# Dense passes in fp32 instead of two fp32r halves, and layer 2's counted nodes from 2304 to 2560

## The chip, the core and the metric

The kernel runs on one core of a Trainium2 chip. TensorE (PE in the profile, its weight loads PEld) multiplies, VectorE (DVE) and ScalarE (ACT) work element by element, GpSimd (POOL) issues the gathers of rows by index, and SyncE (SP) issues the plain transfers. The time is device microseconds of one execution, and a comparison is made on medians of several runs.

## The reference

A two-layer GraphSAGE network with a residual layer norm, on 12500 nodes of 256 features and 200000 edges that are sorted by destination:

```python
def _sage_conv(x, src, dst, W_l, b_l, W_r):
    msgs = x[src]
    agg = jax.ops.segment_sum(msgs, dst, num_segments=N_NODES)
    deg = jax.ops.segment_sum(jnp.ones((src.shape[0],), x.dtype), dst, num_segments=N_NODES)
    mean = agg / jnp.maximum(deg, 1.0)[:, None]
    return mean @ W_l + b_l + x @ W_r

h = jax.nn.relu(_sage_conv(x, src, dst, W1_l, b1, W1_r))
h = jax.nn.relu(_sage_conv(h, src, dst, W2_l, b2, W2_r))
return _layernorm(x + (h @ W3 + b3))
```

Destinations are drawn as `12500 * u**2`, so low-numbered nodes have many more edges than high-numbered ones.

## The kernel before, in words

All 12500 nodes stand in 98 blocks (NB) of 128. The edges stand in 1563 tiles of 128. Sums over edges are made in two ways.

**Gathered nodes.** For nodes from HOT1 = 1792 on (layer 1) or HOT2 = 2304 on (layer 2), a round of `Gathers` (line 258) issues four indirect DMAs on POOL (line 286), one tile of edges each; four products with 0/1 matrices (line 298, 32 output rows each) sum the rows, and for each group of one or two rounds two further products (line 314) put the sums at their nodes, and VectorE adds them to a ring of sums (line 328).

**Counted, or hot, nodes.** For the nodes below that, the kernel counts how often each of the 12500 source nodes occurs for each of 512 or 256 hot nodes: `count` (line 881) makes 0/1 matrices on VectorE (lines 898, 908), multiplies them on TensorE in bf16 (lines 930, 934) and copies the result as bytes (line 944 on ScalarE, line 948 on VectorE). COUNTED (line 109) lists the six groups of nodes. A dense pass, `products` (line 841), then multiplies all rows of x (or h) by such a table: for each of 98 blocks, ScalarE widens the counts from bytes (`widened`, line 833), SP loads the block's rows (`loaded`, line 775), and TensorE accumulates over all blocks in PSUM. A full pass is 512 columns wide, with one PSUM bank for each half of the features (dense_ps and beside_ps, line 868); a half pass is 256 wide (line 864).

**Exactness.** Before, the dense passes multiply in the fp32r form, and each row of x and h is split in two parts for it: the upper 20 bits of each word, by an integer mask of -4096, and the rest, by a subtraction. The products of both parts are added in PSUM, which is 2 parts x 2 halves of the features, four matmuls a block. x is split by `splitting` (line 784) in layer 1's first stage: SP loads two blocks, VectorE masks and subtracts (lines 812 and 813), SP stores them to x2_d. h is split in each `first_block` by `exact` (line 758, called at 1184) and stored to h2_d, beside h itself in h_d. Dense passes read x2_d and h2_d, 256 KB a block.

**Order.** PE and POOL run in an order written out by hand in `layer` (line 645). It loops over the gather rounds; after each round's gathers it lets pieces of finished blocks pass (`pieces`: transposes, line 1094; the two weight products, lines 1123 and 1125; in layer 2 also line 1207) and fills with dense work (`fill`) until the planned cost of the round reaches `room_for`. The planned cost of one block of a dense pass is `product_cost` (line 993); counts, gathers and blocks have planned costs as well. `stages_1` and `stages_2` (lines 1055 and 1067) say which passes, counts and moves are mixed in which stage: layer 1 has one half pass (nodes 1536 to 1791) and three full ones, layer 2 four full ones and one half (2048 to 2303). When the fill is used up, the last rounds run without it, `left` of them, and the last blocks are drained.

The split stage of layer 1 mixes three things: the counts of group 3, `degrees`, and `splitting`.

Of the kernel before, what the change touches and what calls it, by code (L numbers as in the profile page):

```python
# [8 lines left out]
F32 = mybir.dt.float32  # L9
F32R = mybir.dt.float32r  # L10
# [17 lines left out]
P = 128  # L28
# [23 lines left out]
def by_runs(  # L52
# [56 lines left out]
    COUNTED = [(0, 512), (512, 1024), (1024, 1536), (1536, 1792), (1792, 2048), (2048, 2304)]  # L109
    HOT1, HOT2, N1 = 1792, 2304, 4  # L110
# [32 lines left out]
    x2_d = dram.tile([P, NB, 2, D], F32, name="x2_d")  # L143
    h2_d = dram.tile([P, NB, 2, D], F32, name="h2_d")
# [473 lines left out]
    split = keep.tile([P, 2, 2, D], F32, name="split")  # L618
    assert NB * CW % 4 == 0
    counts_flat = [keep.tile([P, NB * CW], U8, name=f"counts{i}") for i in range(2)]  # L620
    counts = [t.rearrange("p (b d) -> p b d", b=NB) for t in counts_flat]
# [151 lines left out]
    N2, WIDE = 5, 4  # L773

    def loaded(b, back, table):

        rows = rows_pool.tile([P, 2, D], F32, name="rows", bufs=N2)
        load = nc.sync.dma_start(rows, table[:, b])
        freed(load, back)
        if table is h2_d:  # L780
            tc.add_manual_dep(load.ins, rows_after, LANDED, reason="the first layer's last gathers")
        return rows

    def splitting():

        size = 2 * 2 * D
        bufs = NB * CW // 4 // size
        flat = counts_flat[1].bitcast(F32)
        raw = {}

        def fetched(u):
            t = flat[:, u // 2 % bufs * size:(u // 2 % bufs + 1) * size].rearrange("p (b k d) -> p b k d", b=2, k=2)
            whole = min(2, (N - u * P) // P)
            loads = []
            if whole < 2:
                left = N - (u + whole) * P
                nc.vector.memset(t[:, whole, 1], 0.0)
                loads.append(nc.sync.dma_start(t[:left, whole, 1], x[(u + whole) * P:N]))
            if whole:
                loads.append(nc.sync.dma_start(t[:, :whole, 1], x[u * P:(u + whole) * P].rearrange(  # L800
                    "(b p) d -> p b d", p=P)))
            if u < 2 * bufs:
                for load in loads:
                    tc.add_manual_dep(load.ins, strips[-1], LANDED, reason="the gathers' tables first")
            return t

        for b in range(0, NB, 2):
            for u in range(b, min(b + 2 * (bufs - 3), NB), 2):
                if u not in raw:
                    raw[u] = fetched(u)  # L810
            s = raw.pop(b)
            nc.vector.tensor_scalar(s[:, :, 0].bitcast(I32), s[:, :, 1].bitcast(I32), -4096, None, op0=OP.bitwise_and)
            nc.vector.tensor_tensor(s[:, :, 1], s[:, :, 1], s[:, :, 0], op=OP.subtract)
            nc.sync.dma_start(x2_d[:, b:b + 2], s)
            yield COST_SPLIT
# [17 lines left out]
    def widened(counted):  # L833
        wide = rows_pool.tile([P, DN], F32, name="wide", bufs=WIDE)
        if len(counted.shape) > 2:
            nc.scalar.copy(wide.rearrange("p (b d) -> p b d", b=2).bitcast(F32R), counted)
        else:
            nc.scalar.copy(wide.bitcast(F32R), counted)  # L838
        return wide
# [777 lines left out]
```

## Time and profile before

| what | value |
|---|---|
| median of 3 runs | 3097.36 us (3088.63 to 3106.94) |
| the profiled execution's own time | 3104.8 us |
| its span | 3103.0 us |
| mean granted TensorE clock | 0.897 |
| gathers issued on POOL | 988 in layer 1, 908 in layer 2 |
| moved by DMA | 634.88 MB, 205 GB/s on the mean |

The page gives the busy time of each engine, then slices of the span with a digit for the busy share in tenths, then the chain of waits followed back from the last instruction. In a row of a group, the count (x) is of records in the trace, then busy time and the mean length of one, then the engine's idle time before them and what ended it. A matmul's length holds the run through the array as well, so matmuls that follow one another overlap, and the price of one in a stream is the distance between two starts. A row of windows gives, for each stretch, its length, each engine's busy time with the count of instructions, the granted clock as a share of the full one, and the share of DMA time.

### The profile page before, as it was taken

The page shows a single profiled execution, that of the slowest core. Times are in us where ns is not written, and L with a number is a line of the kernel's source. Part 1 is how long each engine was busy: PE and PEld are TensorE (multiplying, and loading weights), DVE is VectorE, ACT ScalarE, POOL GpSimd, SP SyncE. Part 2 cuts the span into 40 slices and gives each one's busy share as a digit, 9 for nine tenths or more (in the row PEclk, how much of TensorE's full clock was granted, in tenths as well). Part 3 has the DMA queues.
Part 4 walks back from the last instruction along what each step waited for, and adds up shares of the span by engine and source line. Part 5 has one row for each costly group of instructions (what it writes and reads, how often), then busy time and mean ns, then how long its engine had stood idle before and what let it go on. Part 6 is the DMA issues. An engine that isn't in the chain of part 4 may idle for free.

```text
span 3103.0 us, 45692 instructions
## 1 busy us (share of the span) xinstructions
PE 2412.6 (78%) x13753; PEld 1604.2 (52%) x13753; DVE 1525.2 (49%) x4554; ACT 1384.4 (45%) x2794; POOL 1851.4 (60%) x1906
## 2 busy tenths in 40 slices
PE   3356888888878788888876888887888888887776
PEld 1123555555544555556554555554555566566644
DVE  6764766656666666643232124444444343344344
ACT  0236666666622666644332443554444423333321
POOL 6546666556655666656654665665666556666653
PEclk7567999999999999989988998998998899989988
DMA  4893877756655555567756875766677657677843
GB/s 116 301 348 109 260 228 232 252 183 200 188 183 164 174 165 177 170 187 245 241 178 198 258 229 177 219 215 184 209 226 230 192 173 219 212 222 236 263 130 90
DMA packets 366615, 634.88 MB, mean 205 GB/s; under 512 B 85371, under 2 KB 173081, under 8 KB 366361
## 3 DMA queue, kind: packets, MB, share of 16 engines
q1 hardware_dynamic: 271011, 382.42, 38.3%
q0 software_dynamic: 91008, 248.63, 26.7%
q8 instruction: 115, 1.88, 0.2%
q10 hardware_dynamic: 4342, 0.80, 0.2%
q14 instruction: 139, 1.14, 0.1%
HBM read 544.85 MB, written 86.78 MB: 204 GB/s over the span
## 4 chain that ended last, share of the span: by engine, by line
PE 63%; issue 9%; DVE 8%; another core or an unknown queue 7%; DMA 6%; ACT 5%; DVEq 1%; POOL 0%; ACTq 0%; SPq 0%; POOLq 0%
PE dense_ps L868 10%; PE beside_ps L868 10%; PE count_ps L930 9%; PE part_ps L298 8%; PE block_ps L1123 5%; PE block_ps L1125 5%; PE sum_ps L314 5%; PE block_ps L1207 3%; PE block_ps L1094 3%; ACT counts L944 3%; PE dense_ps L864 3%; PE count_ps L934 2%; DMA rows<-h_d 2%; DMA x_d<-counts 1%
## 5 line engine op out<-in xcount | busy, mean ns | idle before, releaser
L286 POOL DMA_INDIRECT got<-in_x_dram,src_t x988 | 983.6, 996 | 646.1 <-issue 241.3
L286 POOL DMA_INDIRECT got<-h_d,src_t x908 | 865.6, 953 | 573.9 <-issue 226.4
L930 PE MATMUL count_ps<-pick,low 128*128 128x490 bf16 x1360 | 453.8, 376 | 333.8 <-ACT counts L944 139.1
L944 ACT CAST counts<-count_ps 128x490 f32 (+2 forms) x852 | 581.2, 682 | 232.3 <-PE count_ps L934 52.4
L868 PE MATMUL dense_ps<-wide,rows 128*128 128x512 f32 x1372 | 637.7, 465 | 46.5 <-ACT wide L838 16.3
L868 PE MATMUL beside_ps<-wide,rows 128*128 128x512 f32 x1372 | 565.7, 412 | 0.0
L838 ACT CAST wide<-counts 128x512 fp32r<-128x512 uint8 x588 | 359.6, 621 | 455.8 <-PE beside_ps L868 188.9
L868 PEld LDWEIGHTS dense_ps<-wide,rows 128*128 128x128 f32 x1372 | 276.6, 202 | 187.3 <-issue 99.5
L908 DVE TENSOR_SCALAR pick<-steps,tables 128x686 bf16<-128x686 f16 (+3 forms) x792 | 319.0, 416 | 105.2 <-PE count_ps L930 38.6
L298 PE MATMUL part_ps<-got,one 128*32 128x257 f32 (+1 forms) x3792 | 331.7, 424 | 22.8 <-DMA got<-h_d,src_t 12.4
L930 PEld LDWEIGHTS <-low 128*128 128x128 bf16 x1360 | 152.0, 117 | 318.2 <-issue 161.6
L948 DVE CAST counts<-count_ps 128x196 f32 (+2 forms) x316 | 208.5, 660 | 179.8 <-PE count_ps L930 46.9
L868 PEld LDWEIGHTS beside_ps<-wide,rows 128*128 128x128 f32 x1372 | 275.8, 201 | 40.1 <-ACT split L876 0.3
L308 ACT COPY some<-part_ps 128x257 f32<-128x257 f32 (+1 forms) x340 | 127.0, 374 | 351.1 <-PE part_ps L298 102.9
L314 PEld LDWEIGHTS sum_ps<-two,some 128*128 128x128 f32 x1360 | 223.7, 215 | 89.4 <-issue 39.4
L242 DVE TENSOR_TENSOR one<-lo_t,lane_b 128x128 f32<-128x128 bf16 x474 | 134.8, 286 | 267.1 <-PE part_ps L298 81.6
L314 PE MATMUL sum_ps<-two,some 128*128 128x128 f32 x1360 | 238.7, 303 | 32.2 <-ACT some L308 12.8
L328 DVE TENSOR_TENSOR sums<-sums,sum_ps 128x256 f32 x340 | 139.7, 411 | 250.0 <-PE beside_ps L868 88.7
L1133 DVE TENSOR_TENSOR own<-block_ps,biases 128x256 f32<-128x256 f32 x196 | 82.9, 423 | 312.3 <-remote 101.8
L298 PEld LDWEIGHTS part_ps<-got,one 128*32 128x32 f32 x3792 | 78.5, 112 | 191.1 <-issue 167.9
L934 PE MATMUL count_ps<-aft,low 128*128 128x98 bf16 x659 | 169.0, 256 | 0.0
L1130 ACT COPY sums<-zero 128x256 f32<-128x256 f32 x164 | 66.4, 405 | 224.6 <-PE block_ps L1125 74.3
(199 smaller groups left out, 2904.8 us busy)
## 6 DMA issues: line engine op xcount, KB each, us to landing
rows<-h_d SPq DMA_DIRECT2D x490, 256.0 KB
rows<-x_d SPq DMA_DIRECT2D x392, 256.0 KB
x_d<-counts SPq DMA_DIRECT2D x49, 512.0 KB
h_d<-split SPq DMA_DIRECT2D x98, 256.0 KB
got<-in_x_dram,src_t POOLq DMA_INDIRECT x988
got<-h_d,src_t POOLq DMA_INDIRECT x908
h_d<-own SPq DMA_DIRECT2D x98, 128.0 KB
h_sb<-h_d SPq DMA_DIRECT2D x98, 128.0 KB
```

The source lines that it names most:

```text
L286: rows = nc.gpsimd.indirect_dma_start(out=g[:, j, :D], out_offset=None, in_=self.table, in_offset=bass.IndirectOffsetOnAxis(ap=src_t[:, e: ...
L298: strip = nc.tensor.matmul(part_ps[j * W:(j + 1) * W, :width], lhsT=one[:, j], rhs=g[:, j, :width], start=r == 0, stop=r == n - 1)
L314: nc.tensor.matmul(sum_ps[:, c], lhsT=some[:, c * P:(c + 1) * P], rhs=two, start=True, stop=True)
L838: nc.scalar.copy(wide.bitcast(F32R), counted)
L868: nc.tensor.matmul(ps[c], lhsT=own, rhs=wide[u].bitcast(F32R), start=u + k == 0, stop=u == NB - 1 and k == 1)
L908: nc.vector.tensor_scalar(r[:, :w * NB], steps[:, :w * NB], key_t[g][:, t - lo_g:t - lo_g + 1], None, op0=OP.is_equal)
L930: nc.tensor.matmul(ps[:, :(b - a) * NB], lhsT=s, rhs=r[:, a * NB:b * NB], start=j == 0, stop=j == n_in - 1 and alone)
L934: nc.tensor.matmul(ps[:, :NB], lhsT=before[0], rhs=before[1], start=False, stop=True)
L944: copies.append(nc.scalar.copy(to[:, :, a:][:, :, bass.ds(off_act.at(t), b - a)], of).ins)
L948: beside.append(nc.vector.tensor_copy(to[:, :, a:][:, :, bass.ds(off_dve.at(t), b - a)], of).ins)
L1123: nc.tensor.matmul(ps[:, 1], lhsT=own_t[:, c], rhs=wr[:, c], start=c == 0, stop=c == NC - 1)
L1125: product = nc.tensor.matmul(ps[:, 0], lhsT=agg[:, c], rhs=wl[:, c], start=c == 0, stop=c == NC - 1)
```

## The change

- The dense passes read x and h_d themselves and multiply in fp32: two matmuls a block in place of four, with no cast to fp32r on either operand. The rows come two blocks to one transfer of 256 KB (five such pairs ahead).
- `splitting`, `exact` and both tables x2_d and h2_d go, with their VectorE operations, loads and stores. The count tables need no flat form any more, and `sums_b` and `w3_sb` get tiles of their own.
- The last group of counted nodes is 2048 to 2559, and HOT2 is 2560: layer 2's last pass is a full one of 512 columns, and layer 2 has fewer gather rounds.
- The planner's costs change: a product block 1.0 to 0.87 (half pass 0.6 to 0.45), the last piece of `first_block` 1.65 to 0.9 on VectorE, and `room_for` 5.05 to 4.65 in layer 1 and 5.0 to 5.05 in layer 2.

```diff
-    COUNTED = [(0, 512), (512, 1024), (1024, 1536), (1536, 1792), (1792, 2048), (2048, 2304)]
-    HOT1, HOT2, N1 = 1792, 2304, 4
+    COUNTED = [(0, 512), (512, 1024), (1024, 1536), (1536, 1792), (1792, 2048), (2048, 2560)]
+    HOT1, HOT2, N1 = 1792, 2560, 4
...
-    def exact(t, s):
-
-        nc.vector.tensor_scalar(s[:, 0].bitcast(I32), t.bitcast(I32), -4096, None, op0=OP.bitwise_and)
-        nc.vector.tensor_tensor(s[:, 1], t, s[:, 0], op=OP.subtract)
...
-    N2, WIDE = 5, 4
+    PAIRS_IN, WIDE = 5, 4
-    def loaded(b, back, table):
-
-        rows = rows_pool.tile([P, 2, D], F32, name="rows", bufs=N2)
-        load = nc.sync.dma_start(rows, table[:, b])
-        freed(load, back)
+    def loaded(u, since, table):
+
+        rows = rows_pool.tile([P, 2, D], F32, name="rows", bufs=PAIRS_IN)
...
+            loads.append(nc.sync.dma_start(rows[:, :whole], table[u * P:(u + whole) * P].rearrange(
+                "(b p) d -> p b d", p=P)))
+        for load in loads:
+            freed(load, since - (u - 2 * PAIRS_IN + 1))
...
-            nc.scalar.copy(wide.bitcast(F32R), counted)
+            nc.scalar.copy(wide, counted)
...
             for u in (b, b + 1):
-                for k in range(2):
-                    for c in range(NC):
-                        own = rows[u][:, k, c * P:(c + 1) * P].bitcast(F32R)
...
-                            nc.tensor.matmul(ps[c], lhsT=own, rhs=wide[u].bitcast(F32R),
-                                             start=u + k == 0, stop=u == NB - 1 and k == 1)
+                for c in range(NC):
+                    own = rows[b][:, u - b, c * P:(c + 1) * P]
...
+                        nc.tensor.matmul(ps[c], lhsT=own, rhs=wide[u], start=u == 0, stop=u == NB - 1)
...
-        on_pe, on_act = (1.0, 0.62) if width == DN else (0.6, 0.33)
+        on_pe, on_act = (0.87, 0.62) if width == DN else (0.45, 0.33)
...
-        yield [counting(3), (degrees(HOT1 // P), 12.0), (splitting(), NB // 2 * max(COST_SPLIT))]
+        yield [counting(3), (degrees(HOT1 // P), 12.0)]
...
-        yield [passed(waiting, 2048, 256, held(1, 256), h2_d, into)]
+        yield [passed(waiting, 2048, 512, held(1), h_d, into)]
...
         nc.sync.dma_start(h_d[b * P:(b + 1) * P, :], h)
-        s = split[:, b % 2]
-        exact(h, s)
-        nc.sync.dma_start(h2_d[:, b], s)
-        yield 1.75, 1.65, 1.1
+        yield 1.75, 0.9, 1.1
...
-        layer(gathers_1, first_block, 3, staged(stages_1), 5.05, 8)
+        layer(gathers_1, first_block, 3, staged(stages_1), 4.65, 8)
...
-    layer(Gathers(h_d, True), last_block, 5, staged(stages_2), 5.0, 14)
+    layer(Gathers(h_d, True), last_block, 5, staged(stages_2), 5.05, 14)
```

More of the change, by code (lines that the diff above doesn't have):

```diff
@@ L616, in by_runs @@
     keep = ctx.enter_context(tc.tile_pool(name="keep", bufs=1))
[L618 to L621, printed above, removed]
+    sums_b = keep.tile([P, NC, 256], F32, name="sums_b")
+    w3_sb = keep.tile([P, NC, D], F32, name="w3_sb")
+    counts = [keep.tile([P, NB, CW], U8, name=f"counts{i}") for i in range(2)]
     HELD = [counts[1], counts[0], counts[1], counts[0], counts[0][:, :, 256:], counts[1]]
@@ L850, in products @@
         for b in range(0, NB, 2):
-            for u in range(b, min(b + N2, NB)):
+            for u in range(b, min(b + 2 * PAIRS_IN, NB), 2):
                 if u not in rows:
-                    rows[u] = loaded(u, b - (u - N2), table)
+                    rows[u] = loaded(u, b, table)
+            for u in range(b, min(b + 6, NB)):
+                if u not in counted:
                     counted[u] = counts_of(u) if not half or u % 2 == 0 else None
```

84 lines of the change are left out of this document (30 added, 54 removed).

## The prediction

> **What bounds the kernel now.** I read the page first: its busy shares, its slices, its chain.
>
> ```profile
> span 3103.0 us, 45692 instructions
> PE 2412.6 (78%) x13753; PEld 1604.2 (52%) x13753; DVE 1525.2 (49%) x4554; ACT 1384.4 (45%) x2794; POOL 1851.4 (60%) x1906
> PE   3356888888878788888876888887888888887776
> ...
> PE 63%; issue 9%; DVE 8%; another core or an unknown queue 7%; DMA 6%; ACT 5%; DVEq 1%; POOL 0%; ACTq 0%; SPq 0%; POOLq 0%
> ```
>
> TensorE is the busiest engine, at eight tenths in nearly every slice after the third, and carries 63% of the chain of waits; POOL, which issues all gathers, carries none of it. Next I cut the span at the gather rounds where the stages change (the build's order of instructions says which round begins a stage; four L286 issues make a round).
>
> ```profile
> core 0: us, PE busy (x) PEld busy (x) DVE busy (x) ACT busy (x) POOL busy (x), PEclk, DMA share, GB/s
> 0.00:68.80 68.80, 24.98 (x132) 13.68 (x132) 45.07 (x169) 2.78 (x5) 43.65 (x46) 0.78 0.50 117
> 68.80:279.50 210.70, 103.92 (x671) 52.42 (x671) 131.99 (x346) 79.95 (x139) 118.91 (x108) 0.62 0.73 267
> ...
> 1305.80:1558.30 252.50, 215.60 (x1164) 149.39 (x1164) 95.88 (x324) 110.33 (x244) 151.74 (x160) 0.92 0.70 221
> 1558.30:1658.80 100.50, 73.54 (x386) 49.48 (x384) 44.87 (x153) 29.10 (x82) 42.56 (x44) 0.86 0.58 181
> ...
> 1820.60:2112.60 292.00, 238.92 (x1286) 161.38 (x1285) 123.09 (x338) 135.10 (x267) 176.07 (x185) 0.91 0.68 207
> ...
> 2931.00:3103.00 172.00, 118.41 (x658) 81.69 (x656) 74.15 (x228) 37.19 (x106) 87.15 (x92) 0.86 0.42 124
> ```
>
> Where dense passes run, TensorE idles about 1 us a round: (252.5 - 215.6) / 40 rounds = 0.9, and (292.0 - 238.9) / 46 = 1.15. A round there takes about 6.3 us. POOL could do one in 5.0:
>
> ```profile
> 2299.34 0.95 POOL L286 DMA_INDIRECT got<-h_d,src_t  x1 [0.30 <-issue]
> 2302.18 0.94 POOL L286 DMA_INDIRECT got<-h_d,src_t  x1 [1.88 <-PE beside_ps L868]
> 2303.42 0.95 POOL L286 DMA_INDIRECT got<-h_d,src_t  x1 [0.30 <-issue]
> ```
>
> (0.95 + 0.30) x 4 = 5.0, and the longer pause waits for TensorE. So in the dense stages TensorE's own stream of matmuls sets the round. The one other regime is 68.8 to 279.5, where TensorE is half idle and no dense product runs: there the split of x is made.
>
> **The change, part by part. The price of a product.** These rows have the records of both kinds of matmul:
>
> ```profile
> L868 PE MATMUL dense_ps<-wide,rows 128*128 128x512 f32 x1372 | 637.7, 465 | 46.5 <-ACT wide L838 16.3 <-issue 12.1 <-DMA rows<-x_d 7.1
> L868 PE MATMUL beside_ps<-wide,rows 128*128 128x512 f32 x1372 | 565.7, 412 | 0.0
> L864 PE MATMUL dense_ps<-wide,rows 128*128 128x256 f32 x784 | 146.9, 314 | 14.2 <-DMA rows<-h_d 10.2 <-ACT wide L836 2.0 <-issue 1.9
> L1123 PE MATMUL block_ps<-w1r_sb,own_t 128*128 128x256 f32 x392 | 116.8, 425 | 9.0 <-DVE sums L328 4.0 <-remote 3.9 <-issue 0.6
> L314 PE MATMUL sum_ps<-two,some 128*128 128x128 f32 x1360 | 238.7, 303 | 32.2 <-ACT some L308 12.8 <-issue 8.7 <-DVE sums L328 5.5
> ```
>
> Count them against the program. The fp32r products of 7 passes of 98 blocks are 4 matmuls a block, 2744, and there are 1372 + 1372 records: one each. L1123 issues 2 fp32 matmuls for each of 98 blocks of layer 1, and has 392 records: **a true fp32 matmul is two records**. L314 has 1360 for 340 groups of 2: two again. Their lengths overlap, so the price is read from start to start, where the clock is full:
>
> ```profile
> 1400.23 1.02 PE L1123 MATMUL block_ps<-w1r_sb,own_t 128*128 128x256 f32 x4
> 1401.09 1.03 PE L1125 MATMUL block_ps<-w1l_sb,sums 128*128 128x256 f32 x4
> 1401.95 0.61 PE L314 MATMUL sum_ps<-two,some 128*128 128x128 f32 x4
> ...
> 1402.64 0.50 PE L868 MATMUL dense_ps<-wide,rows 128*128 128x512 f32 x1
> ...
> 1403.77 0.64 PE L298 MATMUL part_ps<-got,one 128*32 128x257 f32 x8
> 1404.34 0.50 PE L868 MATMUL dense_ps<-wide,rows 128*128 128x512 f32 x1
> ...
> 1407.24 0.61 PE L314 MATMUL sum_ps<-two,some 128*128 128x128 f32 x4
> ```
>
> Four fp32 records of 256 columns take 0.86 us (1400.23 to 1401.09), 0.215 each, so 0.43 a matmul. A lone fp32r block costs 1.13 us (1402.64 to 1403.77), three in a row 2.90 (1404.34 to 1407.24), 0.97 each. I take their mean, 1.05, over the mean granted clock of the dense rows, about 0.92: **1.135 us a block**.
>
> An fp32 matmul of 512 columns is in no row. Doubling the price of 256 columns gives 0.86, so 1.72 for a block's two. From the other side, if width were free the two would cost what two of 256 columns do, 0.86; but L314's four records of 128 columns end 0.61 after the first start, which with a last record of about 0.3 leaves some 0.11 a record, half of 0.215, so time goes with columns, and I take the upper end. The diff's planner holds 0.87 a block, which is a figure for ordering work and measured by no row; it is a rival below. Over a clock of about 0.945, a little higher because TensorE pauses less, a block costs **1.82 us**.
>
> The Trainium skill, "FP8 and Floating Point Precision", section TensorE Precision Notes, says that true fp32 makes four passes through the array. An estimate from it and the full 2.4 GHz of that skill gives 4 x 512 columns, 0.85 us a matmul, 1.71 a block; the 256-column rows agree with it, and no run shows 512 yet. It speaks against the change and against the planner's 0.87.
>
> - The 686 full blocks of before: 686 x (1.82 - 1.135) = +470 us.
> - Layer 2's last pass becomes a full one: 98 x 1.82 = +178.
> - Its half pass goes, and layer 1's half pass becomes fp32:
>
> ```profile
> 2752.02 1.19 PE L864 MATMUL dense_ps<-wide,rows 128*128 128x256 f32 x8
> 2753.05 0.68 PE L314 MATMUL sum_ps<-two,some 128*128 128x128 f32 x4
> ```
>
> Two half blocks take 1.03, 0.52 each, about 0.6 with switches and clock: 196 x 0.6 = 118 go, and 98 x 0.86 / 0.945 = 89 come. Net -29.
> - The last count group goes from 56 edge tiles to 92.
>
> ```profile
> 1097.65 0.40 PE L930 MATMUL count_ps<-pick,low 128*128 128x490 bf16 x1
> 1097.88 0.25 PE L934 MATMUL count_ps<-aft,low 128*128 128x98 bf16 x1
> 1097.96 0.39 PE L930 MATMUL count_ps<-pick,low 128*128 128x490 bf16 x1
> ```
>
> A tile with one L930 costs 0.31 from start to start; these late tiles have a second one of nearly that width, so 0.5, bounds 0.3 and 0.7: +18.
> - Layer 2 gathers 10 rounds fewer (227 to 217): eight L298 records cost 0.57 (1403.77 to 1404.34), and five groups about 0.5 each: -8.
>
> TensorE's work grows by 470 + 178 - 29 + 18 - 8 = **+629 us**, bounds +520 (clock 1.0, before at 1.13) to +750 (overhead in proportion).
>
> **What goes.** The split of x and of h leaves VectorE and the queues:
>
> ```profile
> L813 DVE TENSOR_TENSOR counts<-counts 128x512 f32<-128x512 f32 x49 | 32.4, 682 | 0.0
> L812 DVE TENSOR_SCALAR counts<-counts 128x512 int32<-128x512 int32 x49 | 21.5, 442 | 30.6 <-DMA counts<-in_x_dram 20.6 <-issue 5.3 <-DMA x_d<-counts 4.6
> ...
> PE count_ps L930 <- DVE pick L908: 48.0, 10, 22.8
> ```
>
> The first two are VectorE's rows between 68.8 and 279.5, the third a wait of TensorE there: VectorE's queue stands behind the split's transfers, and TensorE behind VectorE's picks. In the after program the stage spans 17 rounds (9 to 26), not 27. TensorE idled 210.7 - 103.9 = 107 there; I take 50 afterwards, -57 (bounds -20 to -85), and -15 for records that run less often at the 0.62 clock. The split of h in each first_block (two VectorE operations) is off the path, because VectorE is at 49%; so is the traffic:
>
> ```profile
> DMA packets 366615, 634.88 MB, mean 205 GB/s; under 512 B 85371, under 2 KB 173081, under 8 KB 366361
> ...
> rows<-h_d SPq DMA_DIRECT2D x490, 256.0 KB
> rows<-x_d SPq DMA_DIRECT2D x392, 256.0 KB
> x_d<-counts SPq DMA_DIRECT2D x49, 512.0 KB
> h_d<-split SPq DMA_DIRECT2D x98, 256.0 KB
> ```
>
> Row loads halve per pass and both split stores vanish. TensorE waits for these rows about 24 us by its row of waits above (7.1 + 10.2 and little more), which is inside the next term. A row load is now one transfer for two blocks, ten blocks ahead; its release still waits on the same products, and the count loads behind it on SP have slack.
>
> **What the longer stream covers.** Idle is 3103.0 - 2412.6 = 690. Of it 107 is the split stage; 44 + 27 + 54 = 125 lie in the first, fourth and last rows above, where no dense work runs, and stay. The other 458, 1.1 a round in 420 rounds, are waits of TensorE for ScalarE's copies and VectorE's block steps. The longer products give both engines time to catch up. It can give back nothing (the waits follow a fresh result) or nearly everything; between them I take 0.65 a round over 415 rounds, near the best stage shown (0.9) but with products 1.6 times longer: 270, so **-190 us**.
>
> Sum, against the profiled execution's own time of 3104.8 (1.8 us lie around its span): 3105 + 629 - 57 - 15 - 190 = 3472. The median of the runs, 3097.4, is 7 below that execution: 3465. Both softest terms, clock and catch-up, were taken cautiously, so I say **3450**. Its own range is 3290 to 3590.
>
> **The rivals.**
> 1. *512 columns at the planner's price.* If an fp32 block costs 0.87, it is 0.92 over the clock: dense work becomes 784 x 0.92 + 98 x 0.48 = 768 against 779 + 118 = 897. With +10 for counts and gathers, -72 for the split stage and -10 for ten rounds' idle: 3103 - 129 + 10 - 72 - 10 = 2902, less 6: 2895, faster. It decides if a record of 512 columns starts 0.22 after the last; the rows of 128 and 256 columns speak against it. 9%.
> 2. *TensorE never waits again in dense stages*: all 458 go. 3103 + 629 - 72 - 458 - 6 = 3195. POOL would allow it: 455 rounds x 5.0 = 2275. Against it: waits that follow a result do not shrink. 8%.
> 3. *The clock rises to full.* Granted clock goes with business: 0.62 in the half-idle stage, 0.92 in dense ones. At 1.0 products save 784 x 0.10 = 78 and the other 1500 us of TensorE about 100: 3270. The Trainium skill, "TensorE: Matmul & The Clock Gate", Part 1, says that the throttled state is the default and activity releases it; by that rule this is the case, and the rows so far agree in direction only. 11%.
> 4. *Nothing is covered.* Idle per round stays: 3103 + 629 - 72 - 6 = about 3650. For it: dense-poor and dense-rich stages idle alike, 0.9 and 1.15. 10%.
>
> **How the numbers follow.** The forecast has 62%. The range 3230 to 3630 leaves out rival 1, most of 2 and half of 4, about 19%. Half a per cent is what a measurement of this kernel can tell from no change. Faster is rival 1, 0.08; same 0.01, a fall between it and the rest; slower 0.91.
>
> **What would show it.** The product line should have 3136 records of 512 columns, 0.43 us apart, and their lengths near 0.6; 0.22 apart means rival 1. TensorE's busy time should be near 3000 us, over 85% of the span; POOL's waits for TensorE should grow to rounds of 7 us or more; VectorE's busy should fall; transfers should fall from 635 MB to about 455 (441 row loads of 256 KB fewer, all of the two stores, 49 loads). The stage before the first dense product should end near 190 us, not 280. I am wrong if idle outside setup stays near 460, or falls under 150.

## The result: 4.4% slower

Measured beside each other, before took 3102.15 us and the changed kernel **3233.66 us** (medians of 4 runs each, 3228.92 to 3249.93 for the latter): ratio 1.0437, 95% interval 1.0381 to 1.0493. The forecast was 3450 in a range of 3230 to 3630. The direction was right and the size was not: +353 forecast, +132 measured.

Three conventions for what follows. "Idle" is the span less PE's busy time. Stages are cut at the same gather rounds in all kernels: rounds 0, 9, 36 (27 rounds with the split) or 26 (17 without it), then the stages with dense products, then layer 2 from round 247. And kernels were run in groups, each group on one chip together with the kernel before, and every ratio is taken within its group, because the time of the kernel before turned out to differ between groups: 2607 to 2609 us in some (below: groups of the first kind), 3066 to 3102 in others (of the second kind), never both in one. The first comparison is of the second kind.

The page of the changed kernel, against the one of before:

```profile
span 3227.1 us, 44430 instructions
PE 2927.4 (91%) x13760; PEld 1577.6 (49%) x13760; DVE 1491.8 (46%) x4356; ACT 1459.6 (45%) x2852; POOL 1804.2 (56%) x1866
PE   3579989999888999899979999999999999999996
DMA packets 323044, 449.55 MB, mean 139 GB/s; under 512 B 74581, under 2 KB 262511, under 8 KB 322799
PE 84%; issue 4%; DVE 3%; ACT 3%; another core or an unknown queue 1%; DMA 1%; DVEq 0%; ACTq 0%; POOL 0%; POOLq 0%
```

TensorE went from eight tenths to nine in most slices, and from 63% of the chain of waits to 84%; the share of "another core or an unknown queue" fell from 7% to 1%. Traffic fell from 635 to 450 MB, and the time did not follow it. PE's busy time rose by 2927.4 - 2412.6 = 515 us, and its idle fell by (3103.0 - 2412.6) - (3227.1 - 2927.4) = 690 - 300 = 390. The two make the 124 us between the spans.

The products are what was forecast. Two rows of their group (shortest, median and longest in ns, first and last start), and a stretch of PE's own timeline (start and length in us, and the count):

```profile
L838 PE MATMUL dense_ps<-wide,rows x1568: 590/592/1222, 458.2 to 3118.0; 128*128 128x512 f32 x196
L838 PE MATMUL beside_ps<-wide,rows x1568: 592/592/1061, 459.2 to 3118.8; 128*128 128x512 f32 x196
```

```profile
2004.28 1.02 PE L838 MATMUL dense_ps<-wide,rows 128*128 128x512 f32 x2
2005.14 1.02 PE L838 MATMUL beside_ps<-wide,rows 128*128 128x512 f32 x2
2006.00 1.02 PE L838 MATMUL dense_ps<-wide,rows 128*128 128x512 f32 x2
2006.86 1.02 PE L838 MATMUL beside_ps<-wide,rows 128*128 128x512 f32 x2
2007.81 0.42 PE L295 MATMUL part_ps<-got,one 128*32 128x256 f32 x4
```

There are 3136 records, 592 ns long in the median; a matmul's two take 0.86 us from start to start, 0.43 each, and a block 1.72 (2004.28 to 2006.00). That is the upper of the two prices that the prediction weighed, and the one it took. The estimate by the Trainium skill, "FP8 and Floating Point Precision", TensorE Precision Notes (four passes, 0.85 us), agrees with this 0.86.

Where the idle went shows in the windows (length; busy time with records for PE, PEld, DVE, ACT, POOL; granted clock, DMA share, GB/s):

```profile
66.90:194.60 127.70, 76.65 (x517) 35.41 (x518) 84.74 (x222) 54.43 (x90) 69.71 (x68) 0.61 0.27 78
194.60:1596.20 1401.60, 1277.14 (x6376) 703.31 (x6375) 742.12 (x2220) 741.49 (x1408) 825.27 (x848) 0.98 0.47 138
1596.20:1688.20 92.00, 78.27 (x367) 46.27 (x365) 32.32 (x110) 29.64 (x78) 34.13 (x36) 0.93 0.43 127
1688.20:3096.20 1408.00, 1375.57 (x5842) 715.72 (x5843) 523.31 (x1445) 598.68 (x1180) 773.07 (x808) 0.99 0.51 150
```

The two stretches with dense products in the kernel before, from the profile ahead of the prediction:

```profile
279.50:1558.30 1278.80, 1059.46 (x6211) 687.51 (x6204) 753.07 (x2299) 726.34 (x1400) 780.73 (x800) 0.94 0.65 201
1658.80:2931.00 1272.20, 1032.27 (x5707) 719.42 (x5708) 476.01 (x1362) 509.03 (x1065) 778.45 (x817) 0.91 0.69 215
```

The split stage, 210.7 us with 107 idle, is 127.7 with 51: -56. The two stretches with dense products had 219 + 240 = 459 us idle and now have 124 + 32 = 157: -302, not -190. The rest (start, end of layer 1, tail) went from 124 to 92. And the granted clock in layer 2 rose from 0.91 to 0.99.

### The profile page after: what moved, and what is told of

Read it like the earlier page. It is cut to its first block, busy times and chain, and to the rows that moved or that the text cites. A ratio compares the mean times of both kernels' runs of the same rounds, so it can differ in the third digit from the quotient of the medians.

```text
span 3227.1 us, 44430 instructions
## 1 busy us (share of the span) xinstructions
PE 2927.4 (91%) x13760; PEld 1577.6 (49%) x13760; DVE 1491.8 (46%) x4356; ACT 1459.6 (45%) x2852; POOL 1804.2 (56%) x1866
## 4 chain that ended last, share of the span: by engine, by line
PE 84%; issue 4%; DVE 3%; ACT 3%; another core or an unknown queue 1%; DMA 1%; DVEq 0%; ACTq 0%; POOL 0%; POOLq 0%
PE dense_ps L838 21%; PE beside_ps L838 21%; PE count_ps L899 9%; PE part_ps L295 8%; PE block_ps L1092 5%; PE block_ps L1094 5%; PE sum_ps L311 4%; PE block_ps L1173 3%; PE block_ps L1063 3%; PE dense_ps L834 2%; ACT counts L913 2%; PE count_ps L903 2%; PE sum_ps L317 1%; DVE counts L917 1%
## 5 line engine op out<-in xcount | busy, mean ns | idle before, releaser
L283 POOL DMA_INDIRECT got<-h_d,src_t x868 | 830.5, 957 | 703.4 <-PE part_ps L295 434.6
L838 PE MATMUL dense_ps<-wide,rows 128*128 128x512 f32 x1568 | 828.9, 610 | 8.1 <-ACT wide L807 8.0
L838 PE MATMUL beside_ps<-wide,rows 128*128 128x512 f32 x1568 | 808.7, 598 | 0.0
L807 ACT CAST wide<-counts 128x512 f32<-128x512 uint8 x686 | 422.4, 618 | 741.7 <-PE beside_ps L838 557.8
L899 PE MATMUL count_ps<-pick,low 128*128 128x490 bf16 (+2 forms) x1432 | 447.8, 363 | 152.9 <-ACT counts L913 56.4
L838 PEld LDWEIGHTS beside_ps<-wide,rows 128*128 128x128 f32 x1568 | 300.6, 192 | 380.8 <-issue 380.7
L917 DVE CAST counts<-count_ps 128x196 f32 (+2 forms) x374 | 246.7, 660 | 208.1 <-PE count_ps L899 80.1
L295 PE MATMUL part_ps<-got,one 128*32 128x257 f32 (+1 forms) x3712 | 308.4, 405 | 26.5 <-DMA got<-in_x_dram,src_t 12.5
L311 PEld LDWEIGHTS sum_ps<-two,some 128*128 128x128 f32 x1340 | 202.2, 197 | 101.3 <-issue 76.5
L311 PE MATMUL sum_ps<-two,some 128*128 128x128 f32 x1340 | 213.2, 283 | 13.5 <-DVE own L1103 4.2
```

Of the source, the lines that this page charges most:

```text
L283: rows = nc.gpsimd.indirect_dma_start(out=g[:, j, :D], out_offset=None, in_=self.table, in_offset=bass.IndirectOffsetOnAxis(ap=src_t[:, e: ...
L295: strip = nc.tensor.matmul(part_ps[j * W:(j + 1) * W, :width], lhsT=one[:, j], rhs=g[:, j, :width], start=r == 0, stop=r == n - 1)
L311: nc.tensor.matmul(sum_ps[:, c], lhsT=some[:, c * P:(c + 1) * P], rhs=two, start=True, stop=True)
L807: nc.scalar.copy(wide, counted)
L838: nc.tensor.matmul(ps[c], lhsT=own, rhs=wide[u], start=u == 0, stop=u == NB - 1)
L899: nc.tensor.matmul(ps[:, :(b - a) * NB], lhsT=s, rhs=r[:, a * NB:b * NB], start=j == 0, stop=j == n_in - 1 and alone)
```

## The experiments

### One part of the change at a time

Four kernels were run together beside the kernel before. First, the changed kernel without its other half, with 256 nodes in the last group instead of 512:

```diff
+    COUNTED = [(0, 512), (512, 1024), (1024, 1536), (1536, 1792), (1792, 2048), (2048, 2304)]
+    HOT1, HOT2, N1 = 1792, 2304, 4
...
+        yield [passed(waiting, 2048, 256, held(1, 256), h_d, into)]
```

> Fp32 passes without the split, as changed, but with layer 2's counted nodes back at 2304 and its last pass a half one. Theory (TensorE's stream sets the time, a product block costs what its columns cost): TensorE loses 98 x 0.9 us of products and 18 of counts and gains 10 gather rounds, about -95 us: near 3140 us, with idle near 300. Rival (2560 pays for itself because ten rounds go): 3230 or more.

Then the kernel before with that half alone (the mirror of this edit: `(2048, 2560)`, `HOT2 = 2560`, `passed(waiting, 2048, 512, held(1), h2_d, into)`):

> The kernel before, with layer 2's counted nodes at 2560 alone. Theory: a full fp32r block costs 1.14 against 0.6 for a half one, +52, counts +18, ten rounds -8, part of it covered: 3120 to 3165 us. Rival (the ten gather rounds of 6.2 us go): 3040 to 3060.

The kernel before with its split, its stores and its row loads of both parts, but true fp32 products, of the upper part alone:

```diff
-                for k in range(2):
+                for k in range(1):
...
-                        own = rows[u][:, k, c * P:(c + 1) * P].bitcast(F32R)
+                        own = rows[u][:, k, c * P:(c + 1) * P]
...
-                            nc.tensor.matmul(ps[c], lhsT=own, rhs=wide[u].bitcast(F32R),
+                            nc.tensor.matmul(ps[c], lhsT=own, rhs=wide[u],
...
```

> The kernel before (2304) with the split, its stage, both tables and all their traffic kept, but the passes multiply the upper part alone, in fp32: two matmuls a block, TensorE's work as in the changed kernel. The lower part of x and h is left out of the products. Theory 1 (longer products alone cover the waits): TensorE busy near 2840, idle outside the split stage near 200, in all 3200 to 3250 us, granted clock near 0.96. Theory 2 (the traffic and VectorE's split made the waits): idle stays near 670, 3450 to 3520 us.

And the reverse: the row loads and the planner's figures of the changed kernel, 2304 nodes and no split, but four fp32r matmuls a block. It loads its rows from a plain copy of x that it makes first, and its sums come out doubled and rounded:

```diff
-                        own = rows[u][:, k, c * P:(c + 1) * P].bitcast(F32R)
+                        own = rows[b][:, u - b, c * P:(c + 1) * P].bitcast(F32R)
...
-        yield [counting(3), (degrees(HOT1 // P), 12.0), (splitting(), NB // 2 * max(COST_SPLIT))]
+        for r0 in range(0, N, 14 * P):
+            r1 = min(r0 + 14 * P, N)
+            nc.sync.dma_start(x_c[r0:r1], x[r0:r1])
...
+        yield [counting(3), (degrees(HOT1 // P), 12.0)]
```

> No split (one plain copy of x in DRAM takes its place), rows loaded once in pairs as in the changed kernel, 2304 nodes, but four fp32r matmuls a block as before, both pairs with the unsplit rows, so the sums come out doubled and rounded. Theory 1 (products cover): TensorE busy near 2400, idle outside the first two stages still near 450, 3000 to 3030 us, clock near 0.9. Theory 2 (traffic and split made the waits): idle falls by 300 and more, 2700 to 2750 us.

| kernel | median us | ratio to before (95%) | PE busy | idle |
|---|---|---|---|---|
| fp32_with_split | 3109.91 | 1.1913 (1.1884 to 1.1942) | 2829.2 | 286 |
| fp32_2304 | 3091.56 | 1.1849 (1.1821 to 1.1877) | 2836.2 | 253 |
| split_2560 | 2652.4 | 1.0161 (1.0137 to 1.0185) | 2291.8 | 361 |
| fp32r_no_split | 2596.68 | 0.9953 (0.9935 to 0.9971) | 2258.4 | 341 |
| before, same group | 2606.61 | | | |

The kernel before took 2607 us here, not 3102, so the expected times, which stood on 3102, can't be held against these. Against it the fp32 price alone costs +503 us. Taking the split and its traffic away, with the planner's new figures, gives only 18 in fp32 and 10 in fp32r. The larger last group costs 46 where products are fp32r.

### Is it the chip?

Both kernels were run once more, unchanged, in a group of their own.

> The kernel before, unchanged, with a profile, because it takes 2607 us beside the first four runs and took 3102 us beside the changed kernel. If the chip makes the difference, it is 2600 to 2615 us again with TensorE busy near 2290 us, idle near 310 and granted clock 0.95; the extra 500 us of the first profile are then gaps in which all engines stand still together, and slower records. If the first four runs' kernels disturbed it, it is near 3100.

> The changed kernel, unchanged, beside the kernel before in the same chip time. From fp32_2304 (3092) plus 98 x 0.88 us of products, 18 of counts, less 10 gather rounds of TensorE: 3175 to 3235 us, so 1.22 to 1.24 times the kernel before if that takes 2607; a ratio near 1.044 if the kernel before is at 3100 again.

The kernel before took 2607.83 us (ratio to its companion 0.9996, 0.9982 to 1.001), the changed one 3104.05 (1.1904, 1.1867 to 1.1941). So the same change costs 19% here and 4.4% there. For the changed kernel 3175 to 3235 was expected: what its larger last group adds to fp32_2304 was put too high. The page of the kernel before, as it ran here:

```profile
span 2606.9 us, 45692 instructions
PE 2245.9 (86%) x13753; PEld 1518.6 (58%) x13753; DVE 1527.6 (59%) x4554; ACT 1408.2 (54%) x2794; POOL 1866.1 (72%) x1906
PE 59%; DMA 12%; DVE 6%; ACT 5%; issue 4%; POOL 2%; DVEq 1%; ACTq 0%; SPq 0%; POOLq 0%
```

"Another core or an unknown queue", 7% in the first profile, is not in this chain at all, which could be followed back over 89% of the span. Its split stage and its two stretches with dense products:

```profile
65.27:270.60 205.33, 101.50 (x688) 50.48 (x691) 134.24 (x354) 84.72 (x147) 119.15 (x108) 0.63 0.75 274
270.60:1360.30 1089.70, 998.21 (x6191) 657.34 (x6184) 751.22 (x2291) 729.97 (x1392) 792.33 (x800) 0.98 0.76 236
1436.93:2467.09 1030.16, 951.80 (x5717) 679.80 (x5717) 479.44 (x1364) 524.60 (x1067) 780.87 (x817) 0.98 0.84 266
```

and of the changed kernel here, the same two stretches:

```profile
192.36:1503.14 1310.78, 1252.15 (x6376) 695.36 (x6375) 740.76 (x2219) 745.01 (x1408) 828.64 (x849) 0.99 0.50 148
1585.88:2975.94 1390.06, 1368.68 (x5842) 714.14 (x5843) 523.19 (x1445) 599.06 (x1180) 771.77 (x809) 1.00 0.51 152
```

The split stage of before is what it was (205.3 against 210.7). Its dense stretches are not: 1090 + 1030 us against 1279 + 1272, with 91.5 + 78.4 = 170 us idle against 459, and a clock of 0.98 against 0.94 and 0.91. The 204 rounds of layer 2 take 1030.16 / 204 = 5.05 us each, against 1272.2 / 204 = 6.24. And 5.05 is POOL's own pace, with no wait between the gathers:

```profile
1799.59 0.95 POOL L286 DMA_INDIRECT got<-h_d,src_t  x1 [0.30 <-issue]
1800.84 0.95 POOL L286 DMA_INDIRECT got<-h_d,src_t  x1 [0.30 <-issue]
1802.09 0.94 POOL L286 DMA_INDIRECT got<-h_d,src_t  x1 [0.30 <-issue]
1803.33 0.95 POOL L286 DMA_INDIRECT got<-h_d,src_t  x1 [0.30 <-issue]
1804.58 1.03 POOL L286 DMA_INDIRECT got<-h_d,src_t  x1 [0.30 <-issue]
```

So here layer 2 of the kernel before runs at POOL's pace, with TensorE close behind (951.8 of 1030 us busy). The changed kernel's 202 rounds take 6.88 us here (1390.06 / 202) and 6.97 there (1408 / 202). In layer 2, rounds that are long for TensorE lose almost nothing in the group of the first comparison, and the shorter ones are stretched to 6.2 or so. In the dense stretch of layer 1 the changed kernel loses too: 1401.6 against 1310.8 us, where the kernel before goes from 1089.7 to 1278.8.

### Where is the time lost in groups of the second kind?

The two ideas: TensorE's backlog (a long queue of fp32 work hides late signals), or the split's traffic (twice the row loads, slowed where memory is shared). Two single edits first. The changed kernel with the planner told the measured price, and rooms to match:

```diff
-        on_pe, on_act = (0.87, 0.62) if width == DN else (0.45, 0.33)
+        on_pe, on_act = (1.75, 0.62) if width == DN else (0.88, 0.33)
...
-        layer(gathers_1, first_block, 3, staged(stages_1), 4.65, 8)
+        layer(gathers_1, first_block, 3, staged(stages_1), 5.9, 8)
...
-    layer(Gathers(h_d, True), last_block, 5, staged(stages_2), 5.05, 14)
+    layer(Gathers(h_d, True), last_block, 5, staged(stages_2), 7.2, 14)
```

> The changed kernel with its planner told what the trace of it shows: a product block 1.75 (half pass 0.88) in place of 0.87 (0.45), and room_for 5.9 and 7.2 so that the fill still ends with the gathers. Theory (TensorE is full, so the order of its work is worth little): within 1% of the changed kernel, 3075 to 3135 us where that takes 3104. Rival (rounds overfilled by too low a price starve the gathers and blocks): 2950 to 3040.

and the kernel before with less work for TensorE in layer 2, 2048 counted nodes (no last pass, no last group of counts) and room 4.3 for 5.0:

```diff
+    COUNTED = [(0, 512), (512, 1024), (1024, 1536), (1536, 1792), (1792, 2048)]
+    HOT1, HOT2, N1 = 1792, 2048, 4
...
```

> The kernel before in the other direction: layer 2's counted nodes 2048, so the half pass and the last count group go and 8 more gather rounds come; room_for of layer 2 is 4.3 to spread the fill. Theory (TensorE sets the time): less 98 x 0.63 of products and 56 tiles x 0.5 of counts, plus 8 rounds x 0.85: -80 us of TensorE's work, of which the shorter cover gives some back: 2530 to 2590 us where the kernel before takes 2607. Rival (POOL's 5.0 us a round becomes the bound): 2600 to 2650.

Their group was of the second kind (before: 3065.61). true_prices took 3227.93 us (ratio 1.0556, 1.0504 to 1.0608), where the changed kernel took 3233.66 in the first comparison (ratio 1.0437). The time is the same and the ratio is 1.2% worse, so a right price in the planner, with rooms scaled to it, shows no gain; whether it costs something is not settled, because the changed kernel itself was not in this group. split_2048 took 3086.21 (1.0085, 1.0059 to 1.0112): TensorE has 47 us less to do (2365.2 against 2412.6 in the first profile), there are 8 gather rounds more, and the time does not fall. The expected times were for 2607. Its chain, followed back over 72% of the span, has the same unknown releaser as the first profile's:

```profile
PE 49%; issue 7%; another core or an unknown queue 6%; DVE 5%; ACT 3%; DMA 2%; DVEq 0%; SPq 0%; ACTq 0%; POOL 0%; POOLq 0%
```

To tell backlog from traffic, fp32_with_split (long products, all the traffic) and fp32r_no_split (short products, little of it) were run again in two more groups, and the second of these was of the second kind.

> The same program as fp32_with_split (fp32 products of the upper part alone, the split and all its traffic kept). Where the kernel before takes 2607 it is 3110 again. Where that takes 3070 to 3100: if the extra idle there comes with the traffic of the split (635 MB, as in the kernel before), this one has it too, 3500 to 3600 us, idle near 650; if it is filled by longer products, 3220 to 3260, idle near 300.

> The same program as fp32r_no_split (four fp32r matmuls a block on unsplit rows, half the row traffic; sums come out doubled and rounded). Where the kernel before takes 2607 it is 2597 again. Where that takes 3070 to 3100: if the extra idle comes with the traffic, this one has little of it, 2650 to 2750 us, idle near 350; if short fp32r products leave it uncovered, 3040 to 3090, idle near 650.

> The same program as fp32_with_split once more, for a place where the kernel before takes 3070 to 3100 us. There: 3500 to 3600 us and idle near 650 if the extra idle comes with the traffic of the split; 3220 to 3260 and idle near 300 if longer products fill it. Where the kernel before takes 2607: 3110.

> The same program as fp32r_no_split once more (four fp32r matmuls a block on unsplit rows, sums doubled and rounded). Where the kernel before takes 3070 to 3100 us: 2650 to 2750 and idle near 350 if the extra idle comes with the traffic; 3040 to 3090 and idle near 650 if short fp32r products leave it uncovered. Where it takes 2607: 2597.

| kernel | before at 2607 | before at 3067 | lost there |
|---|---|---|---|
| before itself | 2606.96 | 3067.06 | 460 |
| no_split (fp32r) | 2599.51, ratio 0.997 (0.9959 to 0.998) | 3055.78, ratio 0.9956 (0.9923 to 0.9989) | 456 |
| with_split (fp32) | 3113.22, ratio 1.1936 (1.1916 to 1.1956) | 3238.02, ratio 1.0548 (1.0473 to 1.0623) | 125 |

The two pages where before takes 3067, with_split first:

```profile
span 3232.8 us, 45668 instructions
PE 2860.6 (88%) x13753; PEld 1586.7 (49%) x13753; DVE 1541.2 (48%) x4554; ACT 1423.4 (44%) x2794; POOL 1845.3 (57%) x1906
```

```profile
span 3051.5 us, 44196 instructions
PE 2398.5 (79%) x13753; PEld 1597.2 (52%) x13753; DVE 1444.9 (47%) x4300; ACT 1368.1 (45%) x2753; POOL 1842.9 (60%) x1906
```

with_split moves 635 MB and keeps 372 us idle; no_split moves 468 MB and has 653. The traffic theory wanted it the other way round and falls; the idle of with_split was expected near 300. The loss goes with the length of the products and not with the traffic: about 460 us with fp32r, 125 with fp32. Longer products also give TensorE a larger share of the time, and no run here tells these two apart.

### What the planner's figures are worth

The removed split had been forecast at -72 us, and the runs gave -18 and -10. The windows showed the split stage shorter by 83 us in fp32_2304 than in fp32_with_split, and its layer 2 longer by 67 (1509.7 against 1442.3). The next four ran together (before: 2608.87), three of them with the planner's figures of before:

```diff
-        on_pe, on_act = (0.87, 0.62) if width == DN else (0.45, 0.33)
+        on_pe, on_act = (1.0, 0.62) if width == DN else (0.6, 0.33)
...
-        layer(gathers_1, first_block, 3, staged(stages_1), 4.65, 8)
+        layer(gathers_1, first_block, 3, staged(stages_1), 5.05, 8)
...
-    layer(Gathers(h_d, True), last_block, 5, staged(stages_2), 5.05, 14)
+    layer(Gathers(h_d, True), last_block, 5, staged(stages_2), 5.0, 14)
```

> The changed kernel with 2304 counted nodes, once more, as the partner of the next run on the same chip. Where the kernel before takes 2607 us: 3092. Where it takes 3065: about 3220.

> The same kernel with the planner's figures of before (a product block 1.0, a half one 0.6, room 5.05 and 5.0). Theory A, the prices finish the dense products too early in layer 2 and leave the last 50 or so rounds to POOL: the last dense product moves from 294 us before the end to about 125, layer 2 gets about 50 us shorter, and the time is 30 to 60 us under the partner (near 3045 where before takes 2607). Theory B, the row loads in pairs cost it: the tail moves, but the time stays within 10 us of the partner.

> The fp32r products on unsplit rows (no split, plain copy of x, sums doubled and rounded), with the planner's figures of before. Theory A: 30 to 60 us under the 2598 of the same kernel with the new figures where before takes 2607, so 2540 to 2570, and the split's own worth in fp32r is 40 to 70 us. Theory B: 2590 to 2605.

> The whole change (2560 nodes) with the planner's figures of before. Here dense products last nearly to the end with either figures, so theory A expects little: within 15 us of the changed kernel (3104 where before takes 2607, about 3230 where it takes 3065). Theory B: the same. More than 30 us either way would say that the order matters in some other place.

| kernel | new figures | figures of before |
|---|---|---|
| fp32, 2304 nodes | 3090.83 | 3080.76 |
| fp32r on unsplit rows, 2304 nodes | 2597 and 2600 (earlier groups) | 2608.33 |
| fp32, 2560 nodes | 3104.05 (earlier group) | 3162.72 |

In the sum neither theory held. With the figures of before, fp32 with 2304 nodes gained 10 us, which is no more than theory B allowed and less than the 30 to 60 of A; fp32r lost 9 to 12, where A expected a gain and B at most 7; and the whole change lost 59, where at most 15 was expected. But one half of A held. Layer 2 of fp32_2304_again, then of fp32_2304_old_plan:

```profile
1586.04:3095.00 1508.96, 1405.26 (x6363) 785.28 (x6363) 556.53 (x1586) 570.43 (x1173) 866.97 (x908) 0.97 0.52 153
```

```profile
1644.13:3083.00 1438.87, 1378.62 (x6363) 772.86 (x6363) 557.63 (x1589) 567.50 (x1170) 868.60 (x908) 0.99 0.55 160
```

Layer 2 fell by 70 us, as A expected, because the last dense product starts 128 us before the end and not 293. The rows of the half pass, last start behind "to", new figures first:

```profile
L834 PE MATMUL dense_ps<-wide,rows x784: 377/379/634, 217.2 to 2801.8; 128*128 128x256 f32 x196
```

```profile
L834 PE MATMUL dense_ps<-wide,rows x784: 377/379/796, 218.2 to 2955.3; 128*128 128x256 f32 x196
```

But everything up to layer 2 rose by 58 (1644.13 - 1586.04). Counted in the traces of the 2560 pair, the figures of before finish the products of layer 1 before its last 24 rounds, and the new ones spread them to the last 4. So for 2560 nodes the new figures are worth 59 us (3162.72 - 3104.05, across two groups whose before differ by 1), nearly all in layer 1 (to the start of layer 2, 1641.08 against 1585.88); and with 2304 nodes they give that back in layer 2.

Last, each layer with the figures that suited it in fp32, and the kernel before with the new figures in layer 1 alone. `dense_cost` starts as 0.87 and 0.45, and layer 2 puts the old ones back:

```diff
+    dense_cost[:] = [1.0, 0.6]
+    layer(Gathers(h_d, True), last_block, 5, staged(stages_2), 5.0, 14)
```

> The changed kernel with 2304 nodes, the new planner figures in layer 1 (0.87, 0.45, room 4.65) and those of before in layer 2 (1.0, 0.6, room 5.0). If the layers are independent: layer 1 with 1394 us after its split stage and layer 2 with 1439, so about 3025 where before takes 2608. If they aren't (the order of layer 1 decides what is left for layer 2): 3070 to 3095.

> The kernel before, split and fp32r kept, with the new figures in layer 1 alone. If the new figures are worth what they gave in fp32 (58 us, TensorE's stream being what bounds there): 2550 to 2565 where before takes 2608, a version that beats both. If rounds that POOL already bounds gain less: 2580 to 2600. If the split's VectorE work needs the wider rounds: 2608 or more.

In their group before takes 3102.41. fp32_2304_mixed took 3198.84 (1.0312, 1.0278 to 1.0345), before_mixed 3128.27 (1.0094, 1.0063 to 1.0126). The expected times were for the other kind and can't be held against these. No version with the right sums beat the kernel before: there the new figures cost it 0.9%, and whether the layers can be set apart where it takes 2607 stays open.

## Why the prediction was right in direction and wrong in size

That 3233.66 still lies inside the stated 3230 to 3630 is luck of the place: the forecast was +353, the same change was worth +132 here, and +496 where the kernel before takes 2607.

**The price of a product: right.** A block at 1.72 us of full clock, as taken. Adding in the traces what each product record holds until the next one starts, the products grew from 907 to 1491 us, +585, and where before takes 2607 us from 855 to 1476, +620. The terms 470 + 178 - 29 say 619. That it is priced in time too shows in fp32_with_split: +583 of PE's busy time and +503 us of time. Rival 1, the planner's 0.87, is refuted by the timeline.

**The step that failed: "What the longer stream covers".** Its -190 us measured -302. The prediction called the 458 us of idle in dense stages "waits of TensorE for ScalarE's copies and VectorE's block steps", and let 190 of them go. The split of that number is this:

| idle in dense stages | before | after |
|---|---|---|
| first comparison | 459 | 157 |
| where before takes 2607 | 170 | 80 |
| difference | 289 | 77 |

Of the 459, 289 us are not there when the same program runs in a group of the first kind. They are not waits that the program must make, and by this table, of them 212 went with the change; of the kernel's own 170, 90 went. The forecast of one covering fraction for both was wrong. One row in which such waits were put down to ScalarE is an example (PE's idle before the count products is the number behind the second bar):

```profile
L930 PE MATMUL count_ps<-pick,low 128*128 128x490 bf16 x1360 | 453.8, 376 | 333.8 <-ACT counts L944 139.1
```

```profile
L930 PE MATMUL count_ps<-pick,low 128*128 128x490 bf16 x1360 | 435.0, 368 | 180.9 <-ACT counts L944 87.2
```

The first is the profile that I had, the second the same kernel where it takes 2607: the same work with 153 us less waiting ahead of it.

**The clock: also that step's neighbour.** TensorE's work was forecast at +614 with the cold records (629 - 15), and was +515. The products account for 34 of the 99 missing. About 24 of them are the clock, which the prediction held at 0.945 and which was granted at 0.98 and 0.99 in the dense stages: 784 blocks held 1403 us, 1.79 each and not 1.82. The rest is that the products of before held 907 us where 897 were counted. The other 65 lie in the records that are no products, 1498 us before and 1429 after, where 5 less were forecast (-15 + 18 - 8). That this is the clock too is inferred from their lengths: the largest count products went from 410 to 390 ns, the L314 products from 303 to 283. Together with the idle: 99 + 112 (302 - 190) + 33 (stages where no idle was to go) = 244, less the 1 us by which the split stage missed: 3472 - 243 = 3229, the profiled execution's own 3228.92. (Busy and idle time make up the span, so it must close; what it shows is the size of each miss.) Rival 3 was right in its direction, at 11%, and rival 2 in two thirds of its size (302 gone of 458); the time lies between theirs, 3195 and 3270. The Trainium skill, "TensorE: Matmul & The Clock Gate", Part 1, says that activity releases the throttled clock; the mean granted clock agrees, 0.897 before and 0.967 after, and 0.95 to 0.975 where before takes 2607.

**The split stage: right in its place, wrong as a term of the sum.** Its idle fell by 56 where 57 was forecast, and it ended at 194.6 us where 190 was forecast. But the ten rounds that left it are done later. With the planner's figures held, all of the split's removal is worth 3109.91 - 3080.76 = 29 us in fp32 (across two groups whose before differ by 2), not 72. In fp32r the runs show nothing (2608.33 against 2608.87), but there the plain copy of x stands against it: the first nine rounds of no_split_old_plan end at 91.5 us and those of the kernel before at 65.3, and TensorE waits 30.6 us for gathers there.

**The 512 nodes and the planner.** The larger last group was forecast at 178 - 59 + 18 - 8 = +129 (the half pass of layer 2 is 98 x 0.6 = 59). With the figures of before it costs 3162.72 - 3080.76 = 82, and with the new ones 3104.05 - 3090.83 = 13. The forecast gave the new figures nothing, and they are worth 59 us here. Where before takes 2607 the account is 503 (fp32) - 29 (split) + 82 (nodes) - 59 (planner) = 497. These are steps of one chain of runs, so their sum must meet the 496 between the two medians. They also depend on the order in which they are taken, as the 82 and the 13 show.

**The signs.** PE's busy time near 3000 and over 85%: 2927 and 91%. Idle outside the setup near 460 or under 150 was to make the forecast wrong: it was 157, just inside, though the forecast was 216 us off (3450 - 3234), so that bound told too little. 455 MB: 450. VectorE's busy time fell by 33 us, and POOL waits for TensorE, in rounds of 6.97 us in layer 2 where 7 or more was forecast (6.61 in layer 1's dense stretch, 1401.6 / 212). Its idle before the gathers of layer 2 stands behind the second bar; 434.6 us of it wait for TensorE's part sums, 125.8 before:

```profile
L283 POOL DMA_INDIRECT got<-h_d,src_t x868 | 830.5, 957 | 703.4 <-PE part_ps L295 434.6
```

## What to carry to other kernels

A single profile cannot tell a wait that the program makes from one that the place adds. Before putting a price on idle time, run the unchanged kernel again at another time and place, and distrust idle that comes with "another core or an unknown queue" in the chain, with TensorE, VectorE and ScalarE standing still at once. And price work that moves to another stage there too: a stage that shrinks by 71 us (205.6 to 134.4 with the planner's figures of before) can be worth 29.

## What was not expected of the hardware

**One program, two times.** The kernel before took 2607 to 2609 us on chips numbered 9, 15, 13 and 8, and 3066 to 3102 on those numbered 8, 10 and 0 (the first comparison's number is not on record); number 8 has both, so it is not settled that it belongs to the chip and not to what else ran there. Within a group it didn't change. Of the 496 us between the two profiles of the kernel before, 329 are idle time of TensorE and 167 its busy time, at a granted clock of 0.897 against 0.950; the busy times of VectorE and POOL are the same within 1% (1525.2 and 1527.6, 1851.4 and 1866.1). So most of the time is lost between instructions. The packets of the transfers are not slower: those of the two large DMA queues took 38.3% and 26.7% of 3103 us, and 44.4% and 32.0% of 2607, which is the same time within 3%. This is what it looks like in the timeline of the first profile (in brackets the idle time before, and what ended it):

```profile
899.62 0.95 PE L930 MATMUL count_ps<-pick,low 128*128 128x490 bf16 x3
...
900.94 0.22 PE L320 MATMUL sum_ps<-two,some 128*1 128x128 bf16 x1
...
901.93 0.62 ACT L838 CAST wide<-counts 128x512 fp32r<-128x512 uint8 x1 [3.30 <-issue]
...
902.65 0.95 POOL L286 DMA_INDIRECT got<-in_x_dram,src_t  x1 [0.30 <-issue]
903.31 0.74 DVE L942 TENSOR_TENSOR counts<-counts,count_ps 128x490 f32 x1 [3.16 <-remote]
...
904.33 0.37 PE L930 MATMUL count_ps<-pick,low 128*128 128x490 bf16 x1 [3.17 <-DVE pick L908]
```

TensorE finished its count products at 900.57 and its last product at 901.16, and VectorE's addition of a count product began at 903.31, released by nothing that the profile places; ScalarE and TensorE stood still for over 3 us as well, while POOL went on with its gathers. The traces hold 117 moments of over 0.7 us (198 us in all) in which TensorE, VectorE and ScalarE all stand still in the first profile of before, and 27 (56 us) where it takes 2607; with fp32 products 27 and 8. That fits late signals, which a long queue of products hides, and it fits the stretched rounds.

The traces hold more on this: the times at which semaphores, the signals between engines, were updated. In the example TensorE's update is recorded at 903.29, 2.1 us after its last product, and VectorE starts 0.02 us later. In the first profile 411 of 2808 recorded updates of TensorE's semaphore come over 1 us after the last matmul or weight load that makes one; 216 of these 411 are followed within 0.15 us by a start of VectorE or ScalarE after a pause. Where the kernel before takes 2607, 2 of 3826 come so late. In groups of the second kind there are 486 in no_split, but 131 in the changed kernel and 150 in with_split, the two that lose little. The updates that VectorE and ScalarE make are on time in both kinds (99% within 0.02 us). So TensorE's signals, or the true ends of its matmuls, which the trace only models, come late there. Why stays open, and so does whether the recording of the trace has a part in it: the first profile has 24547 recorded updates in all, the same program 67304 where it takes 2607. Where updates are missing, the engine named as releaser is uncertain, and "another core or an unknown queue" may be no more than such a missing record.

**Half as many matmuls, and over one and a half times the time.** A true fp32 matmul of 512 columns takes 0.86 us in its two records, and an fp32r one 0.24 (0.97 / 4 in a row of blocks), so two of the first cost 1.72 where four of the second cost 0.97 to 1.13.
